# Layer 2's depthwise filter with two accumulators to a step, evictions by rows and a projection in PSUM order

## The chip, the cores and the metric

The kernel runs on one core of one Trainium2 chip. The metric is device time in microseconds of one execution of the whole program, which is four layers long. The change lies in the third of them, called layer 2 in the code. The engines have short names in the profile: PE is TensorE (PEld its weight loads), DVE is VectorE, ACT is ScalarE, POOL is GpSimd and SP is SyncE, which issues the DMAs.

## What is computed

A batch of 32 images of 96 channels and 56 x 56 pixels goes through four residual layers, each behind a group normalisation. Layer 2 is a quantized inverted bottleneck: a 1x1 convolution from 96 to 576 channels, a depthwise 3x3 convolution, and a 1x1 convolution back to 96, with 4-bit weights and activations.

```python
h = bn(conv(x, quant_w(w1, BITW), b1, 1, 0, 1), g1, be1, m1, v1)
h = act_q(h, BITA)
h = bn(conv(h, quant_w(w2, BITW), b2, 1, 1, HID), g2, be2, m2, v2)
h = act_q(h, BITA)
h = bn(conv(h, quant_w(w3, BITW), b3, 1, 0, 1), g3, be3, m3, v3)
return x + h
```

Here `act_q` clips to 0..1 and rounds to fifteenths. The kernel carries the activations as integers 0 to 15 in bf16: an eviction from PSUM applies the folded normalisation and rounds to int16, and a second instruction (`clip`) clamps to 0..15 and turns int16 into bf16 in place.

## The kernel before

The 576 channels of the bottleneck are 18 groups of 32, which make four blocks of four groups and a half block (k = 4) of two. Per image, layer 2 has these steps, each named by a letter.

- `s`, `u`, `v`, `x` and `h`, `y`, `i`, `l`: the image's statistics and normalisation, and its split into three bf16 parts (`hi`, `mid`, `lo`). `h` (L1092) and `i` (L1098) run on ACT; `x` (L1089), `y` (L1095) and `l` (L1101) on DVE. The three parts have one buffer each, so they are an order among themselves: `h`, `y`, `i`, `l`.
- `e` with k and g (expand, L1121): 24 products of a 96 x 32 weight with 392 columns, three parts by two halves by four phases. A phase is one of the four combinations of even and odd rows and columns; phase f goes to PSUM partitions 32f to 32f + 31. So a plane holds, for each group, four phases of 32 channels on 128 partitions. The even and odd halves of its columns lie in the two banks of a PSUM tile.
- `m` with k: the clip of the plane of block k (DVE, L1131).
- `a` with k and i (depthwise, L1151): the filter. A product multiplies all four phases of one group with a 128 x 32 matrix of taps; another half of the products takes only the 64 partitions of the rows above or below. Before the change there are four steps to a block (two halves of the image by even and odd output columns) and two to the half block: 18 steps an image of 32 products each. A step has one PSUM tile; its two banks are even and odd output rows. 16 of its products have 128 rows and 16 have 64.
- `n` with k: the clip of the filtered block (DVE, L1131).
- `j` with i (project, L1169) and `d` with i (add): three projections an image of 40 products, 32 with 128 rows and 8 with the 64 rows of the half block. A PSUM bank is written in the order row, column, column parity, while its layout has the parity outermost. The add is four DVE instructions (L1186) that scale the result into the image.
- `r`, `b`, `o`: residual, its factors, and statistics and store of the result.

The helper `evict` (L1112) empties a PSUM tile after `e` and after `a`: 784 float32 per partition into int16, on ACT or, for steps named in `L2_ON_DVE`, on DVE. That set is empty before.

The order on PE, DVE and ACT is written out by hand: `L2_ORDER` is a string of steps that the program walks once per image. A step with one `-` is done for the image before, with two for the one before that, with `+` for the next. Each engine executes its instructions in this order, and semaphores between them are put in by the framework.

All PSUM of layer 2 is four tiles of two banks each. The helper `bank` hands them out in strict rotation to expand, filter, projection and the two small statistics products, so the fifth request waits until the first tile is emptied. In SBUF there are five planes, six filtered blocks, two of each for the half block, and three pairs of images. After `o` of an odd image, SP stores the pair and then loads the pair after next into the same buffer.

Of the kernel before, what the change touches and what calls it, by code (L numbers as in the profile page):

```python
# [11 lines left out]
BF16 = mybir.dt.bfloat16  # L12
F32R = mybir.dt.float32r
I16 = mybir.dt.int16
# [8 lines left out]
MID = 576  # L23
NBLK = 5
SEH = 24
RT = 7
# [862 lines left out]
class Layer2:  # L889


    def __init__(self, ctx, tc, S, w, y1):
# [21 lines left out]
        def staged(p, n):  # L914
# [2 lines left out]
            return self.pairs[1].rearrange("p r i q -> p (r i q)")[:p, at[0] - n : at[0]]  # L917

        raw = [(name, staged(p, n), tile(f"{name}m", [p, 1]), tile(f"{name}a", [p, 1])) for name, p, n in (
            ("l2_w1", C, MID), ("l2_wphase", 128, NGR * NM), ("l2_w3", 128, NBLK * C))]  # L920
        taps, used, eye4 = raw[1][1], staged(128, NM), staged(128, GC)

        def load():
# [69 lines left out]
def layer2(ctx, tc, S, k2, y1, y2, norm3):  # L993
# [57 lines left out]
    def plane(im, k):  # L1051
        return planes[(CC * im["b"] + k) % L2_PLANES] if k < CC else halfplanes[im["b"] % 2]
# [54 lines left out]
    def evict(out, ps, s, o, c, step):  # L1107

        if step in L2_ON_DVE:
            nc.vector.tensor_scalar(out, ps, s[:, c : c + 1], o[:, c : c + 1], ALU.mult, ALU.add)  # L1110
        else:
            nc.scalar.activation(out, ps, AF.Identity, bias=o[:, c : c + 1], scale=s[:, c : c + 1])  # L1112

    def expand(im, k, g):

        ps, n = bank("ps"), QUAD * k + g
        for part in (hi, mid, lo):
            v = part.rearrange("c (t p r a) q -> c p a t r q", t=NP, p=NPH, a=2)
            for j in range(2):
                for f in range(4):  # L1120
                    nc.tensor.matmul(  # L1121
                        ps[f * GC : (f + 1) * GC, j, :NT].rearrange("p (t r q) -> p t r q", t=NP, q=W4),
                        w1[:, n * GC : (n + 1) * GC], v[:, f % 2 + 2 * j, f // 2],
                        start=(part is hi), stop=(part is lo),
                    )
# [7 lines left out]
    def activate(im, k):  # L1133
        clip(plane(im, k))

    def depthwise(im, k, i):

        half, p = i // 2, i % 2
        parts = [(g, half) for g in range(QUAD)] if k < CC else [(g, h) for h in range(2) for g in range(2)]
        ps, planes = bank("psd"), plane(im, k).rearrange("p g (m q) -> p g m q", q=W2)  # L1140
        q = (-1, 1)[p]
        top, bottom, every = slice(0, HALF), slice(HALF, 128), slice(128)
        rounds = [[(r, 2 * r + p, every, 0, 0)] for r in range(2)] + [[(r, 4 + 2 * r + p, every, 0, q)] for r in range(2)]
        rounds += [[(0, n, bottom, -1, dq), (1, n, top, 1, dq)] for n, dq in ((8 + p, 0), (10 + p, q))]
        n = HH // 2
        for x, products in enumerate(rounds):
            for at, (g, part) in enumerate(parts):
                for r, m, rows, dm, dq in products:
                    r0, r1 = max(part * n, -dm), min((part + 1) * n, HH - dm)
                    q0, q1 = max(0, -dq), W2 - max(0, dq)  # L1150
                    nc.tensor.matmul(  # L1151
                        ps[at * GC : (at + 1) * GC, r, :NT].rearrange("p (r w) -> p r w", w=W2)[
                            :, r0 - part * n : r1 - part * n, q0:q1],
                        filt[rows, (QUAD * k + g) * NM + m, :], planes[rows, g, r0 + dm : r1 + dm, q0 + dq : q1 + dq],
                        start=(x < 2), stop=(x == len(rounds) - 1),
                    )
        evict(act(im, k)[:, half * HH : (half + 1) * HH].bitcast(I16).rearrange("c (m r) (q p) -> c p r m q", r=2, p=2)[:, p],
              ps[:, :, :NT].rearrange("c r (m q) -> c r m q", q=W2), s2, o2, k, f"a{k}{i}")

    def activate2(im, k):  # L1160
        clip(act(im, k))
# [1 line left out]
    def project(im, i):  # L1163
        ps = im["ps"][i] = bank("psj")

        def strip(s, t, k, p, r0, **ends):
            n, c = (i, s) if s < LAST else (LAST, i)
            v = act(im, k)[p, r0 + n // 2 * 2 * RT : r0 + (n // 2 + 1) * 2 * RT]
            nc.tensor.matmul(  # L1169
                ps[s * GC : (s + 1) * GC, t, :NT].rearrange("c (m r q) -> c r q m", m=2, q=W4),  # L1170
                w3[p, k, c * GC : (c + 1) * GC], v.rearrange("p r (q j m) -> p j r q m", j=2, m=2)[:, n % 2], **ends)

        for t in range(2):
            for k in range(CC):
                for s in range(LAST + 1):
                    strip(s, t, k, slice(128), t * HH, start=(k == 0), stop=False)
        for s in range(LAST + 1):
            for t in range(2):
                strip(s, t, CC, slice(t * HALF, (t + 1) * HALF), 0, start=False, stop=True)
# [222 lines left out]
def layouts(a):  # L1402
# [28 lines left out]
    def phase_taps(v):  # L1431
# [43 lines left out]
        "l2_w3": doubled(a[i2 + "w3"].reshape(C, MID).T),  # L1475
# [32 lines left out]
```

## Time and profile before

| | |
|---|---|
| median of three runs | 5905.45 us (5895.33 to 5912.31) |
| the profiled execution | 5899.44 us, span 5897.6 us |
| mean granted TensorE clock | 0.981 |
| PE busy | 5571.7 us, 94% of the span |
| ACT busy | 4501.2 us, 76% |
| DVE busy | 4579.4 us, 78% |
| first and last product of expand (L1121) | 3612.6 and 5375.0 us |
| first and last product of the filter (L1151) | 3653.2 and 5403.9 us |
| last projection (L1169) starts | 5414.8 us |

The span runs from the first to the last instruction. Layer 2 takes roughly 3610 to 5424 us of it; layers 0 and 1 lie before, layer 3 behind. A PE product is shown with a modelled end, and four products for different groups of 32 columns of the array run side by side, so a mean duration of 330 ns says little of the pace; the distances between starts do.

### The profile page before, as it was taken

What the parts mean: (1) busy time and instruction counts of PE and PEld (TensorE: products, weight loads), DVE (VectorE), ACT (ScalarE), POOL (GpSimd) and SP (SyncE); (2) the same over time, 40 slices, a digit from 0 to 9 for tenths busy, and PEclk for the clock granted to TensorE, in tenths of its full rate; (3) what the DMA queues carried; (4) which work ended last, traced back from release to release, by engine and by line L of the source; (5) the groups of instructions that cost most, each with busy time, mean ns of one, the idle gap of its engine ahead of it and who ended that gap; (6) DMA issues with size and microseconds to landing.
All of it is one profiled execution on the core that took longest, in us unless ns stands there. A gap on an engine that the chain in (4) does not pass through costs nothing.

```text
span 5897.6 us, 159737 instructions
## 1 busy us (share of the span) xinstructions
PE 5571.7 (94%) x71208; PEld 2670.0 (45%) x71208; DVE 4579.4 (78%) x4899; ACT 4501.2 (76%) x6036; POOL 260.7 (4%) x141
## 2 busy tenths in 40 slices
PE   5999999999999999996999997999999999996899
PEld 2333333333333333333566664554554555553444
DVE  6999999999999999984766664665666666564777
ACT  5888888888888888864555655888888888895555
POOL 5000000000000000001000000000000000000000
PEclk9999999999999999997999998999999999998999
DMA  3122233322222222236587667467876876745888
GB/s 98 18 56 56 60 62 57 59 58 56 53 56 49 49 53 52 42 26 115 140 154 147 149 148 49 31 40 47 51 41 45 50 44 40 52 31 34 232 251 242
DMA packets 1306642, 455.58 MB, mean 77 GB/s; under 512 B 1123857, under 2 KB 1302025, under 8 KB 1304033
## 3 DMA queue, kind: packets, MB, share of 16 engines
q1 hardware_dynamic: 1305953, 445.36, 50.3%
q8 instruction: 558, 9.14, 0.7%
q14 instruction: 131, 1.07, 0.1%
HBM read 284.26 MB, written 214.08 MB: 84 GB/s over the span
## 4 chain that ended last, share of the span: by engine, by line
PE 88%; DMA 4%; DVE 3%; issue 2%; ACT 1%; SPq 1%; POOL 1%; ACTq 0%; DVEq 0%; POOLq 0%
PE psd L434 17%; PE psd L1151 12%; PE ps L1121 11%; PE psj L485 10%; PE ps L367 7%; PE pc L844 7%; PE pse L390 6%; PE psj L1169 5%; PE pc L1300 3%; PE pc L828 2%; DMA raw<-tdiff 2%; PE pa L802 2%; PE pc L818 1%; DMA X<-y 1%; PE pc L842 1%
## 5 line engine op out<-in xcount | busy, mean ns | idle before, releaser
L408 DVE SCALAR_TENSOR_TENSOR h<-hpad,l_wdw,h 128x3136 f32<-128x3136 f32 x512 | 1782.3, 3481 | 9.1
L434 PE MATMUL psd<-plane,filt 128*32 128x392 f32 (+5 forms) x16384 | 1082.9, 485 | 0.0
L1112 ACT ACTIVATE plane<-ps,o,s 128x784 int16<-128x784 f32 x512 | 601.6, 1249 | 141.3 <-PE ps L1121 136.6
L1151 PE MATMUL psd<-plane,filt 128*32 128x392 bf16 (+5 forms) x16384 | 673.1, 331 | 38.3 <-issue 35.0
L434 PEld LDWEIGHTS psd<-plane,filt 128*32 128x32 f32 (+1 forms) x16384 | 389.7, 108 | 674.6 <-issue 621.8
L1112 ACT ACTIVATE act<-psd,o,s 128x784 int16<-128x784 f32 x512 | 632.5, 1250 | 76.1 <-PE psd L1151 72.4
L674 ACT COPY T<-raw 32x112 f32<-32x112 f32 (+2 forms) x1440 | 463.0, 385 | 286.9 <-DMA raw<-tdiff 231.0
L1121 PEld LDWEIGHTS <-l_w1q 96*32 96x32 bf16 x13824 | 448.4, 95 | 243.0 <-issue 143.8
L1151 PEld LDWEIGHTS <-filt 128*32 128x32 bf16 (+1 forms) x18432 | 312.1, 92 | 453.1 <-issue 390.0
L367 PE MATMUL ps<-xn,l_wboth 96*128 96x392 f32 (+1 forms) x1536 | 465.8, 505 | 23.7 <-ACT xn L349 23.0
L408 DVE SCALAR_TENSOR_TENSOR hc<-hhalf,l_wdw,hc 128x1568 f32<-128x1568 f32 x256 | 473.8, 1851 | 16.1 <-ACT hc L401 9.4
L1300 PE MATMUL pc<-x,T 128*112 128x416 f32 (+1 forms) x1152 | 415.5, 523 | 53.5 <-DMA X<-y 50.7
L844 PE MATMUL pc<-x,T 128*112 128x416 f32 (+1 forms) x1152 | 445.1, 522 | 0.0
L390 PE MATMUL pse<-xn,l_wboth 96*32 96x392 f32 x4096 | 392.4, 501 | 4.6 <-ACT hab L411 4.6
L1121 PE MATMUL ps<-lo,l_w1q 96*32 96x392 bf16 x4608 | 356.3, 337 | 15.9 <-issue 13.1
L1121 PE MATMUL ps<-mid,l_w1q 96*32 96x392 bf16 x4608 | 346.9, 336 | 24.2 <-issue 18.6
L1186 DVE SCALAR_TENSOR_TENSOR xt<-psj,s,xt 32x392 f32<-32x392 f32 (+1 forms) x384 | 223.8, 621 | 177.1 <-PE psj L1169 175.4
L1121 PE MATMUL ps<-hi,l_w1q 96*32 96x392 bf16 x4608 | 339.9, 338 | 21.0 <-issue 13.1
L367 PEld LDWEIGHTS ps<-xn,l_wboth 96*128 96x128 f32 (+1 forms) x1536 | 219.4, 173 | 248.8 <-issue 59.3
L411 ACT ACTIVATE hab<-psd,o,s 128x784 f32<-128x784 f32 x256 | 284.4, 1115 | 58.5 <-PE psd L434 55.6
L1300 PEld LDWEIGHTS pc<-x,T 128*112 128x112 f32 x1152 | 203.7, 177 | 264.8 <-issue 241.4
L377 ACT ACTIVATE hpad<-ps,o,s 128x784 f32<-128x784 f32 x256 | 278.7, 1105 | 49.8 <-PE ps L367 48.5
(233 smaller groups left out, 7843.5 us busy)
## 6 DMA issues: line engine op xcount, KB each, us to landing
X<-y SPq DMA_DIRECT2D x192, 392.0 KB
y<-xt SPq DMA_DIRECT2D x180, 392.0 KB
xt<-in_x_dram SPq DMA_DIRECT2D x16, 2352.0 KB
y<-y SPq DMA_DIRECT2D x96, 392.0 KB
xt<-y SPq DMA_DIRECT2D x96, 392.0 KB
out_dram<-y SPq DMA_DIRECT2D x96, 392.0 KB
twav<-zwav SPq DMA_DIRECT2D x768, 36.8 KB
raw<-twav SPq DMA_DIRECT2D x96, 168.0 KB
```

The source lines that it names most:

```text
L367: nc.tensor.matmul(ps[p, j, :NT], wexp[:, k * 128 : k * 128 + 128][:, m], im["xn"][:, j, rows, :].rearrange("c h w -> c (h w)"), start=Tru ...
L390: nc.tensor.matmul(ps[f * GC : (f + 1) * GC, half, :NT].rearrange("p (r w) -> p r w", w=W2), wexp[:, c : c + GC], im["xn"][:, f % 2, r0 : ...
L408: nc.vector.scalar_tensor_tensor(h2, taken(im, k, t), wdw[:, k, t : t + 1], h2, ALU.mult, ALU.add)
L434: nc.tensor.matmul(ps[at * GC : (at + 1) * GC, r, :NT].rearrange("p (r w) -> p r w", w=W2)[:, r0 - half * n : r1 - half * n, q0:q1], filt[ ...
L485: nc.tensor.matmul(ps[s * GC : (s + 1) * GC, t, :NT].rearrange("c (m r q) -> c r q m", m=2, q=W4), wg[p, k, c * GC : (c + 1) * GC], phases ...
L674: nc.scalar.copy(to.rearrange("x t (p s) -> x t p s", p=NPH), v[:, k])
L844: nc.tensor.matmul(ps[:PH, to], st["T"][j][:, h, k, :], st["x"][:, j, h, of], start=False, stop=(n == NK - 1))
L1112: nc.scalar.activation(out, ps, AF.Identity, bias=o[:, c : c + 1], scale=s[:, c : c + 1])
L1121: nc.tensor.matmul(ps[f * GC : (f + 1) * GC, j, :NT].rearrange("p (t r q) -> p t r q", t=NP, q=W4), w1[:, n * GC : (n + 1) * GC], v[:, f % ...
L1151: nc.tensor.matmul(ps[at * GC : (at + 1) * GC, r, :NT].rearrange("p (r w) -> p r w", w=W2)[:, r0 - part * n : r1 - part * n, q0:q1], filt[ ...
L1169: nc.tensor.matmul(ps[s * GC : (s + 1) * GC, t, :NT].rearrange("c (m r q) -> c r q m", m=2, q=W4), w3[p, k, c * GC : (c + 1) * GC], v.rear ...
L1300: nc.tensor.matmul(ps[:, :, to], st["T"][:, h, k, :], st["x"][:, h, :, of], start=(n == 0), stop=(n == NK - 1))
```

## The change

The third weight gets a sixth block, and zeros are written so that block 4 has values for the upper 64 partitions only and block 5 for the lower 64. The filter step takes a block and a half of the image, both column parities and both row parities: it has two PSUM tiles, one for even and one for odd output rows, and in each a bank for even and one for odd columns. First come 32 products with 128 rows, then 32 with 64 rows, upper and lower in turn. There are two evictions after it, one for each tile, which read the banks in turn and write whole rows. Expand's eviction also reads its two banks in turn and writes contiguously. The projection reads the filtered block in PSUM's order, so that a product's columns are written one after the other, and takes the half block with 128 rows against the zero-filled weights. Four of the 18 expand evictions of an image go to DVE. The hand-written order is another one.

```diff
 L2_ORDER = """
-    n4-- s m3-- m4- n0-- a21-- e21- e00- u e32- e02- n2-- a32-- a33-- e01- e13- v e23- a31-- a30-- e30-
-    e22- n1-- n3-- e11- e20- e03- e12- j2-- e33- r- x m2- e31- m1- h j0-- d2-- a40- m0- d0-- a11- y a03-
-    a41- i j1-- d1-- b a23- a20- a00- a10- a22- l a01- a12- e41 e40 o-- a02- e10 a13-
+    e13- e33- m0- n4-- n1-- n0-- e41- x e20- m2- e11- n3-- e12- v n2-- e30- e40- e10- h m1- a00- a10-
+    j0-- m3- y i d0-- m4- j1-- a01- d1-- j2-- a20- d2-- a21- a30- l e00 a40- e02 r- e03 s+ a31- e01 e31
+    a11- e22 o-- u+ e21 b e23 e32
 """
 L2_PLANES, L2_ACTS = 5, 6
-L2_ON_DVE = set()
+L2_ON_DVE = {"e00", "e10", "e20", "e30"}
...
-        w1, w3 = tile("l2_w1q", [C, MID], BF16), tile("l2_w3q", [128, NBLK, C], BF16)
+        w1, w3 = tile("l2_w1q", [C, MID], BF16), tile("l2_w3q", [128, NBLK + 1, C], BF16)
...
+            nc.vector.memset(w3[64:, CC, :], 0.0)
+            nc.vector.memset(w3[:64, NBLK, :], 0.0)
...
-        evict(plane(im, k)[:, g, :].bitcast(I16).rearrange("p (m q j) -> p j m q", q=W4, j=2),
-              ps[:, :, :NT].rearrange("p j (m q) -> p j m q", q=W4), s1, o1, n, f"e{k}{g}")
+        evict(plane(im, k)[:, g, :].bitcast(I16).rearrange("p (n j) -> p n j", j=2),
+              ps[:, :, :NT].rearrange("p j n -> p n j"), s1, o1, n, f"e{k}{g}")
...
-    def depthwise(im, k, i):
+    def depthwise(im, k, half):
...
+        ps, planes = [bank("psd") for _ in range(2)], plane(im, k).rearrange("p g (m q) -> p g m q", q=W2)
+        n, sides = HH // 2, (slice(HALF, 128), slice(0, HALF))
...
+        banks = [(r, p) for r in range(2) for p in range(2)]
+        for shifted in range(2):
+            for r, p in banks:
+                for at in range(4):
+                    product(r, p, at, 4 * shifted + 2 * r + p, slice(128), 0, (-1, 1)[p] * shifted, start=not shifted)
+        for shifted in range(2):
+            for p in range(2):
+                for at in range(4):
+                    for r in range(2):
+                        product(r, p, at, 8 + 2 * shifted + p, sides[r], (-1, 1)[r], (-1, 1)[p] * shifted, stop=bool(shifted))
+        for r in range(2):
+            v = act(im, k)[:, half * HH + r : (half + 1) * HH : 2].bitcast(I16)
+            evict(v.rearrange("c m (q p) -> c m q p", p=2), ps[r][:, :, :NT].rearrange("c p (m q) -> c m q p", q=W2),
+                  s2, o2, k, f"a{k}{half}{r}")
...
-                ps[s * GC : (s + 1) * GC, t, :NT].rearrange("c (m r q) -> c r q m", m=2, q=W4),
-                w3[p, k, c * GC : (c + 1) * GC], v.rearrange("p r (q j m) -> p j r q m", j=2, m=2)[:, n % 2], **ends)
...
+                    v = act(im, k)[:, r0 : r0 + 2 * RT].rearrange("p r (q j m) -> p j m r q", j=2, m=2)[:, n % 2]
+                    nc.tensor.matmul(
+                        ps[s * GC : (s + 1) * GC, t, :NT].rearrange("c (m r q) -> c m r q", m=2, q=W4),
+                        w3[:, k + t * (k == CC), c * GC : (c + 1) * GC], v, start=(k == 0), stop=(k == CC))
```

`product` in the new filter step is the old inner product: the same tap matrix, the same shifted window of the plane, written to tile `r`, bank `p`, partitions 32 `at` on.

More of the change, by code (lines that the diff above doesn't have):

```diff
@@ L919, in __init__ @@
         raw = [(name, staged(p, n), tile(f"{name}m", [p, 1]), tile(f"{name}a", [p, 1])) for name, p, n in (
-            ("l2_w1", C, MID), ("l2_wphase", 128, NGR * NM), ("l2_w3", 128, NBLK * C))]
+            ("l2_w1", C, MID), ("l2_wphase", 128, NGR * NM), ("l2_w3", 128, (NBLK + 1) * C))]
         taps, used, eye4 = raw[1][1], staged(128, NM), staged(128, GC)
@@ L1134, in activate @@
         clip(plane(im, k))
-    def depthwise(im, k, i):
-        half, p = i // 2, i % 2
+    def depthwise(im, k, half):
         parts = [(g, half) for g in range(QUAD)] if k < CC else [(g, h) for h in range(2) for g in range(2)]
[L1140 to L1158, printed above, removed]
@@ new lines, in depthwise, with product @@
+        ps, planes = [bank("psd") for _ in range(2)], plane(im, k).rearrange("p g (m q) -> p g m q", q=W2)
+        n, sides = HH // 2, (slice(HALF, 128), slice(0, HALF))
+        def product(r, p, at, m, rows, dm, dq, start=False, stop=False):
+            g, part = parts[at]
+            r0, r1 = max(part * n, -dm), min((part + 1) * n, HH - dm)
+            q0, q1 = max(0, -dq), W2 - max(0, dq)
+            nc.tensor.matmul(
+                ps[r][at * GC : (at + 1) * GC, p, :NT].rearrange("p (r w) -> p r w", w=W2)[
+                    :, r0 - part * n : r1 - part * n, q0:q1],
+                filt[rows, (QUAD * k + g) * NM + m, :], planes[rows, g, r0 + dm : r1 + dm, q0 + dq : q1 + dq],
+                start=start, stop=stop)
@@ L1164, in project @@
         ps = im["ps"][i] = bank("psj")
[L1166 to L1169, printed above, removed]
-                ps[s * GC : (s + 1) * GC, t, :NT].rearrange("c (m r q) -> c r q m", m=2, q=W4),
-                w3[p, k, c * GC : (c + 1) * GC], v.rearrange("p r (q j m) -> p j r q m", j=2, m=2)[:, n % 2], **ends)
         for t in range(2):
-            for k in range(CC):
+            for k in range(NBLK):
                 for s in range(LAST + 1):
[L1176 to L1179, printed above, removed]
+                    n, c = (i, s) if s < LAST else (LAST, i)
+                    r0 = t * HH * (k < CC) + n // 2 * 2 * RT
+                    v = act(im, k)[:, r0 : r0 + 2 * RT].rearrange("p r (q j m) -> p j m r q", j=2, m=2)[:, n % 2]
+                    nc.tensor.matmul(
+                        ps[s * GC : (s + 1) * GC, t, :NT].rearrange("c (m r q) -> c m r q", m=2, q=W4),
+                        w3[:, k + t * (k == CC), c * GC : (c + 1) * GC], v, start=(k == 0), stop=(k == CC))
     def add(im, i):
@@ L1474, in layouts @@
         "phase_used": phase_taps(np.ones((GC, 9), np.float32))[:, 0],
-        "l2_w3": doubled(a[i2 + "w3"].reshape(C, MID).T),
+        "l2_w3": doubled(a[i2 + "w3"].reshape(C, MID).T)[:, [0, 1, 2, 3, 4, 4]],
         "l2_mid": np.concatenate([columns([i2 + n + x for n in ("b", "g", "be", "m", "v")], f) for x, f in
```

## The prediction

> **What bounds the kernel now.** I read the page's engine table and slices first, then the three 100 us windows in the middle of layer 2, then the groups of layer 2 by line, and last the timeline of TensorE (PE) over one stretch of an image. The slices show where layer 2 lies: from the 25th to the 37th, where PE and ACT are both high.
>
> ```profile
> PE   5999999999999999996999997999999999996899
> ...
> ACT  5888888888888888864555655888888888895555
> ...
> DMA  3122233322222222236587667467876876745888
> ```
>
> The windows, which show microseconds busy and instructions in brackets, put sizes to it: PE 94%, ACT 87%, DVE 63%, TensorE's clock at full.
>
> ```profile
> 4300.00:4400.00 100.00, 95.86 (x2059) 51.28 (x2053) 67.62 (x98) 87.15 (x70) 1.15 (x1) 1.00 0.84 50
> ...
> sum 300.00, PE 283.24 PEld 149.01 DVE 188.94 ACT 260.39 POOL 5.73; mean PE 94.41 PEld 49.67 DVE 62.98 ACT 86.80 POOL 1.91
> ```
>
> A busy PE is not yet a PE at its peak, so I take its work from distances between starts in the timeline.
>
> ```profile
> 4309.41 2.89 PE L1169 MATMUL psj<-act,l_w3q 128*32 128x392 bf16 x32
> 4312.23 0.52 PE L1169 MATMUL psj<-acth,l_w3q 64*32 64x392 bf16 x8
> 4312.68 1.30 PE L1151 MATMUL psd<-planeh,filt 128*32 128x392 bf16 x32
> ...
> 4320.82 8.72 PE L1151 MATMUL psd<-plane,filt 128*32 128x392 bf16 x224
> 4329.47 0.53 PE L1121 MATMUL ps<-hi,l_w1q 96*32 96x392 bf16 x8
> ...
> 4331.51 1.20 PE L1151 MATMUL psd<-plane,filt 128*32 128x392 bf16 x24
> ```
>
> The reader is to see three paces. Two expand steps (48 products) take 4331.51 - 4329.47 = 2.04 us: 0.170 us for each four products of 392 columns, which run together in four column groups. A projection takes 4312.68 - 4309.41 = 3.27 us for 40 products; its 32 full ones take 2.82 us, 0.352 us for four, twice the pace of expand. Seven filter steps of 32 products take 4329.47 - 4320.82 = 8.65 us, 1.236 us each.
>
> One image of layer 2 is, on PE: 18 expands of 1.02 (18.4), 18 filter steps of 1.236 (22.2), 3 projections of 3.27 (9.8), two small group products (0.5), together 50.9 us. The line of L1092, which runs once per image, starts first at 3615.1 and last at 5320.5: 31 intervals of 55.0 us. So 4.1 us per image are stalls. ACT has per image, from these groups, 1390.0/32 = 43.4 us of evictions (the two below and the two of the half blocks, 80.1 and 75.8), 2.9 of L1092 and 2.8 of L1098: 49.1 us. DVE, summing its layer 2 rows, has 1144/32 = 35.8 us.
>
> ```profile
> L1112 ACT ACTIVATE act<-psd,o,s 128x784 int16<-128x784 f32 x512 | 632.5, 1250 | 76.1 <-PE psd L1151 72.4 <-ACT act L1112 0.3
> L1112 ACT ACTIVATE plane<-ps,o,s 128x784 int16<-128x784 f32 x512 | 601.6, 1249 | 141.3 <-PE ps L1121 136.6 <-ACT act L1112 0.2 <-PE pv L1076 0.2
> L411 ACT ACTIVATE hab<-psd,o,s 128x784 f32<-128x784 f32 x256 | 284.4, 1115 | 58.5 <-PE psd L434 55.6
> ...
> L394 ACT ACTIVATE plane<-pse,o,s 128x784 f32<-128x784 f32 x256 | 256.1, 1001 | 26.2 <-PE pse L390 21.4
> ```
>
> ```profile
> L1186 DVE SCALAR_TENSOR_TENSOR xt<-psj,s,xt 96x392 f32<-96x392 f32 x192 | 110.9, 618 | 175.4 <-PE psj L1169 175.4
> ```
>
> These are groups by shape: busy, mean ns of one, idle time before it and what ended that. ACT and DVE wait for PE here, not PE for them: PE bounds layer 2, ACT is 2 us per image behind it.
>
> [...]only the projection writes PSUM with neighbours far apart (its innermost index steps 196 floats), and only it runs at 0.352 instead of 0.170. [...]a filter step is four quads of full products and two octets of 64-row products, six slots of 0.167 us (1.00 us) if the octets run as one; it takes 1.236, so 0.234 is left for its two changes of mode. [...]the new projection reads bf16 at steps of 8 bytes[...], and no row of before shows such a read. [...]
>
> **The change part by part.**
> Filter steps. Two steps become one of 64 products with two accumulators: eight quads, four octets, one pair of mode changes. 12 x 0.167 + 0.234 = 2.24 us against 2.47, 9 times an image: -2.1 us on the path. The 64-row products run side by side already (unpaired, the step would hold 8 slots, 1.33 us, more than it takes)[...].
> Projection. 40 full products with contiguous writes; the half block's 64-row products become 128-row ones against zeros, eight in two slots, without a change of mode. 10 x 0.167 = 1.67 against 3.27, 3 times: -4.8 us. If the 8-byte reads run at half pace, 10 x 0.33 = 3.3 and the gain is nil[...]. I take full pace, [...]the trace ties the slow pace to the writes.
> PE then: 50.9 - 6.9 = 44.0 us.
> Evictions. Both forms now write int16 rows contiguously (before: every second element) and read the two PSUM banks in turn. Contiguous writing is worth up to 249 ns (1250 against L394). What reading in turn costs no row shows: at the least nothing (1001)[...]. I take 0.1, the price that a strided far side has in L411 (1115 against 1001): 1.1 us. Four of 36 evictions per image go to DVE. ACT: 32 x 1.1 + 5.7 = 40.9 us, where unchanged evictions would give 45.7.
> DVE. Four tensor_scalars of 784 floats from PSUM: from L1186, 618 ns for 392, plus 392 more at 1.04 ns (L408's two sizes, 3481 ns for 3136 and 1851 for 1568), an estimate of 1.03 us[...]. 35.8 + 4.1 = 39.9 us, beside PE. Behind each stand clips, the chain rest and lo, and the projection's adds; e00 stands right behind lo, which PE needs for e00 anyway.
> Banks. A filter step now holds two of the four tiles for 2.24 us and both evictions start at its end, so the second tile is held 2.24 + 2.2 us; before, 1.24 + 1.25. Time that tiles are held per image: before 18 x 2.27 (expand) + 18 x 2.49 + 3 x 5.6 (projection and its adds of 2.35) = 103 of 4 x 55 us; after 18 x 2.1 + 9 x (3.3 + 4.4) + 3 x 4.0 = 119 of 4 x 49. Between the last expand of one image and the first of the next, PE has 6 filter steps and 3 projections, 18.4 us; DVE, from the end of L1092 (2.9), must do L1095 (3.46), three adds of 2.35, a clip and L1101 (3.41), 17.4 us in all. It fits with 1 us to spare; the stretch of before was 20.1 us (two projections, 11 filter steps). For both I add 0.9 us of stalls per image.
> Once-only edits (a wider third weight, two memsets) are under 1 us beside layer 1.
> DMA: a pair's store and load take 4211.45 to about 4282, some 70 us, of the 110 us of two images; at 98 us it still fits.
>
> Sum: 44.0 + 4.1 + 0.9 = 49.0 us against 55.0; 6.0 x 32 images = -192 us. The profiled execution took 5899.4 (span 5897.6), 6 us under the median of 5905.5. 5899.4 - 192 = 5707; I say 5705.
>
> **The rivals.**
> A, the reads of the projection are slow (half pace): PE 48.8, stalls as before, 52.9 us: -2.1 x 32 = -67; with ACT's relief taking a little more, 5820. For it: nothing in before reads so.[...]
> B, the stalls shrink, as ACT is 8 us per image lighter and no longer close behind PE: 44.0 + 2 = 46 us, -288: 5610. For it: ACT, busy 49.1 of 55.0, is the only engine near PE, so its bursts are the nearest cause of PE's stalls. Against: the tiles are held longer.
> C, slower: reading PSUM banks in turn costs ACT more than contiguous writing saves. It decides from (55.0 - 4.1 - 5.7)/32 = 1.41 us an eviction; at 1.55 ACT has 55.3 us, with stalls 59: +4 x 32 = 6030. For it: the 0.25 us that strided writing costs shows that ACT is not indifferent to steps. Against: f32 at 8-byte steps cost only 0.1.
> D, two tiles per filter step starve PE: stalls rise to about 11 us and the interval stays at 55: 5895, no change.
> That the pairs were meant to run together for the first time is excluded above.
>
> **How the numbers follow.** Forecast 0.50, A 0.17, B 0.14, C 0.13, D 0.06. Predicted: 5705. The range reaches from B's side, 5600, to just past A, 5840; C, D and a little of B's tail lie outside. 0.3% (18 us) is about what a measurement of this kernel can tell from no change. Faster: 0.50 + 0.17 + 0.14 = 0.81; same: most of D, 0.04; slower: C and the rest of D, 0.15.
>
> **What would show it.** In the changed profile: four products of L1169's successor at 0.17 us pace, a projection of 1.7 us (A: 3.3); a filter step of 2.2 us with one gap of about 0.1 us before its 64-row part; evictions at 1.0 to 1.15 us (C: over 1.4) and DVE evictions at about 1.0; hi starting every 49 us. PE waiting for evictions rather than the reverse, with ACT under 85%, would show D. The prediction is wrong if evictions come out above 1.3 or the projection above 2.2.

## The result, and the profile after

The changed kernel takes 5930.78 us (median; 5914.36 to 5952.28), the kernel before in the same runs 5911.09 us (5895.33 to 5922.98). The ratio is 1.0039, with a 95% interval of 1.0027 to 1.0051: 0.4% slower, where 3.4% faster was forecast. The profiled execution took 5931.0 us (span 5929.2).

The slices of the page hardly differ for PE and DMA; ACT is lighter in layer 2.

```profile
PE   5999999999999999986999997999899999896899
...
ACT  5888888888888888864565654666566666663455
...
DMA  3122233222222222236576666556956866745888
```

The three windows in the middle of layer 2 for which the prediction shows before (microseconds busy, instructions in brackets; clock, DMA share and GB/s at the end) say the same with sizes.

```profile
4300.00:4400.00 100.00, 92.88 (x2008) 57.80 (x2004) 67.51 (x93) 64.98 (x61) 2.29 (x2) 1.00 0.61 43
...
sum 300.00, PE 277.18 PEld 172.81 DVE 198.72 ACT 189.57 POOL 6.87; mean PE 92.39 PEld 57.60 DVE 66.24 ACT 63.19 POOL 2.29
```

ACT went from 87% to 63%, DVE from 63% to 66%, PE from 94% to 92%. PE runs 2008 products in the first of these windows, before it ran 2059. PE still bounds the layer and waits more often. Each eviction, by shape (busy, mean ns, idle before and what ended it), is as cheap as was hoped:

```profile
L1114 ACT ACTIVATE act<-psd,o,s 128x784 int16<-128x784 f32 x512 | 486.2, 1000 | 412.7 <-PE psd L1148 408.0 <-issue 3.9
L1114 ACT ACTIVATE plane<-ps,o,s 128x784 int16<-128x784 f32 x384 | 376.7, 1005 | 103.2 <-PE ps L1123 96.5
```

1000 and 1005 ns stand against 1250 and 1249; the 128 evictions on DVE (L1112) take 1092. The fault lies on PE. Its timeline (start, length, products in the row) over a projection and over three filter steps:

```profile
4323.81 1.58 PE L1181 MATMUL psj<-act,l_w3q 128*32 128x392 bf16 x16
4325.20 0.54 PE L1181 MATMUL psj<-acth,l_w3q 128*32 128x392 bf16 x4
...
4327.31 1.63 PE L1181 MATMUL psj<-act,l_w3q 128*32 128x392 bf16 x16
...
4336.58 6.87 PE L1148 MATMUL psd<-plane,filt 128*32 128x392 bf16 x192
4343.38 0.53 PE L1123 MATMUL ps<-hi,l_w1q 96*32 96x392 bf16 x8
```

A projection takes 4327.31 - 4323.81 = 3.50 us for 40 products, ten quads (four products side by side) of 0.350 us: the pace of before, not 0.167. Three filter steps of 64 products take 4343.38 - 4336.58 = 6.80, 2.27 us each. PE's work per image is then 18.4 (expand, unchanged) + 9 x 2.27 + 3 x 3.50 + 0.5 = 49.8 us, before 50.9. The line of L1092, now L1094, runs once per image; its row gives shortest, median and longest duration, then first and last start:

```profile
L1094 ACT ACTIVATE hi<-xt,rstd x32: 2897/2917/2931, 3615.4 to 5344.4; 96x3136 bf16<-96x3136 f32 x32
```

That is 1729.0/31 = 55.8 us per image, before 55.0. So 1.1 us of work went and 1.9 us of stalls came: 6.0 us against 4.1. Over 31 intervals +24 us; from the last `hi` to the last projection the pipeline now runs dry in 107.7 us instead of 94.2, another +13. The remainder of the profiled difference, a few us the other way, lies outside layer 2.

What is a stall? The view of PE's waits over 3750 to 5150 us (released by; us in total, times, longest) answers "issue", a wait that no semaphore ends. First before, then after:

```profile
PE ps L1121 <- issue: 37.3, 42, 2.7
PE psd L1151 <- issue: 32.5, 35, 3.0
```

```profile
PE psd L1148 <- issue: 59.2, 42, 4.7
PE ps L1123 <- issue: 37.5, 33, 5.7
...
PE psd L1148 <- DVE plane L1133: 2.7, 17, 0.2
PE psd L1148 <- ACT act L1114: 2.6, 1, 2.6
```

In these rows evictions (L1114) and clips (L1133) hold PE for 5.3 of 1400 us; "issue" holds it for 97, before for 70. Where such waits fall is seen in the timeline:

```profile
4347.84 0.35 PE L1148 MATMUL psd<-planeh,filt 64*32 64x378 bf16 x7 [1.18 <-issue]
4348.12 0.53 PE L1123 MATMUL ps<-hi,l_w1q 96*32 96x392 bf16 x8
...
4349.81 0.58 PE L1123 MATMUL ps<-lo,l_w1q 96*32 96x392 bf16 x8
4350.15 2.38 PE L1148 MATMUL psd<-plane,filt 128*32 128x392 bf16 x64
4352.46 0.53 PE L1123 MATMUL ps<-hi,l_w1q 96*32 96x392 bf16 x8
4352.81 0.33 PE L1123 MATMUL ps<-mid,l_w1q 96*32 96x392 bf16 x1
4355.15 0.53 PE L1123 MATMUL ps<-mid,l_w1q 96*32 96x392 bf16 x7 [2.01 <-issue]
```

Between the two gaps stand 7 + 48 (six rows of expand, of which the first and the last are shown) + 64 + 8 + 1 = 128 products. The second gap cuts a run of eight equal products after the first, where no data can be late. Along the whole layer two gaps are 128 products apart or a multiple of it, give or take the one or two that the trace may miss. A product is two instructions (a weight load and a matmul: 2004 and 2008 of them in the first window above), so 128 are 256 instructions. The page counts PE's instructions and, for one DMA queue of the kind "instruction", packets and MB:

```profile
PE 5563.7 (94%) x71208; PEld 2777.3 (47%) x71208; DVE 4711.7 (79%) x5029; ACT 4119.9 (69%) x5908; POOL 255.5 (4%) x141
...
q8 instruction: 558, 9.14, 0.7%
```

That is 9.14/558 MB = 16.4 KB (16384 bytes) a packet, and 2 x 71208/558 = 255 of PE's matmuls and weight loads to a packet; the other engines together have far fewer instructions than that. So q8's packets are read here as blocks of 256 of PE's instructions, and a gap falls where one block ends; the gaps are up to 5.7 us long. The DMA view of the same window has the blocks (packets, MB, share), and its slices of 2.5 us show when data moves:

```profile
DMA  9000000000000001556545555565555899999999
GB/s 47 4 7 0 7 0 7 0 0 7 0 7 0 0 7 17 59 59 73 64 57 70 62 66 63 61 75 63 67 64 63 95 67 66 70 68 68 62 63 70
...
q1 hardware_dynamic: 35866, 4.00, 59.8%
q8 instruction: 15, 0.25, 1.1%
...
y<-xt SPq DMA_DIRECT2D x6, 392.0 KB
xt<-y SPq DMA_DIRECT2D x5, 392.0 KB
```

Fifteen blocks are what 2008 products need (2008/128 = 15.7). From 4303 to 4337 us no image is moved: the lone sevens are instruction blocks, one every 4 to 8 us, and the products of that stretch, the projections above among them, run without a gap over 0.2 us. From 4338 the store of a pair of images runs, six transfers of 392 KB in a row, and the gaps begin, 6.2 to 7.3 us apart where one comes at each edge.

The trace also has the time of each block. SP issues the second and third of these transfers at 4345.00 and 4351.86 us; blocks start at 4345.49 and 4352.80 and take 0.9 us each, and PE goes on at 4347.84 and 4355.15. Over the whole layer it is the same: every one of the 82 gaps (counted as in the next section) ends 1.2 to 2.5 us after a block has landed, and of the 133 blocks that start while SP is issuing an image transfer (for 6.3 us, as a rule) 110 start in its first 2 us, where chance would give about a third.

A part of the stalls is no wait at all. From the first to the last `hi`, TensorE's granted clock stands at half for 100.6 us in all, before for 39.8. In both, 19 us of that lie at the layer's beginning; the rest comes in stretches of 3.4 or 6.8 us, 16 of them after and 5 before. Four expand products take 0.327 us there instead of 0.170. This is one, with the gap in front of it and a filter step that takes 3.6 us, mostly inside it, and then a window of it (the 0.50 is the clock):

```profile
4404.03 0.85 PE L1148 MATMUL psd<-plane,filt 64*32 64x364 bf16 x28 [2.55 <-issue]
...
4406.11 3.68 PE L1148 MATMUL psd<-planeh,filt 128*32 128x392 bf16 x64
4409.72 0.53 PE L1123 MATMUL ps<-hi,l_w1q 96*32 96x392 bf16 x8
```

```profile
4405.60:4408.80 3.20, 3.20 (x44) 1.83 (x36) 2.37 (x2) 1.22 (x2) 0.00 (x0) 0.50 1.61 67
```

Ten of the 16 begin within 1.6 us after the end of a distance of over 2 us between the starts of two products, the other six in the last 1.7 us of one; past the layer's beginning after has 24 of them. At half clock PE loses half the time: 1.6 us per image after, 0.6 before. So of the 1.9 us by which the stalls grew, about half are gaps (3.0 to 4.0, the table below) and half are clock.

### The profile page after: what moved, and what is told of

The parts are those of the page before. It is cut to its first block, busy times and chain, and to the rows that moved or that the text cites. A ratio compares the mean times of both kernels' runs of the same rounds, so it can differ in the third digit from the quotient of the medians.

```text
span 5929.2 us, 159802 instructions
## 1 busy us (share of the span) xinstructions
PE 5563.7 (94%) x71208; PEld 2777.3 (47%) x71208; DVE 4711.7 (79%) x5029; ACT 4119.9 (69%) x5908; POOL 255.5 (4%) x141
## 3 DMA queue, kind: packets, MB, share of 16 engines
q8 instruction: 558, 9.14, 0.7%
## 4 chain that ended last, share of the span: by engine, by line
PE 86%; DVE 4%; DMA 3%; issue 3%; SPq 2%; ACT 1%; POOL 1%; DVEq 0%; ACTq 0%; POOLq 0%
PE psd L434 17%; PE ps L1123 11%; PE psj L485 10%; PE psd L1148 10%; PE ps L367 7%; PE pc L844 7%; PE pse L390 6%; PE psj L1181 6%; PE pc L1304 3%; PE pc L828 2%; PE pa L802 2%; DMA raw<-tdiff 1%; PE pc L818 1%; DVE h L408 1%; PE pc L842 1%
## 5 line engine op out<-in xcount | busy, mean ns | idle before, releaser
L1114 ACT ACTIVATE act<-psd,o,s 128x784 int16<-128x784 f32 x512 | 486.2, 1000 | 412.7 <-PE psd L1148 408.0
L1148 PE MATMUL psd<-plane,filt 128*32 128x378 bf16 (+5 forms) x16384 | 619.1, 330 | 51.9 <-issue 43.4
L1123 PEld LDWEIGHTS <-l_w1q 96*32 96x32 bf16 x13824 | 475.2, 97 | 227.2 <-issue 137.2
L1148 PEld LDWEIGHTS <-filt 128*32 128x32 bf16 (+1 forms) x18432 | 416.3, 95 | 352.7 <-issue 250.5
L1114 ACT ACTIVATE plane<-ps,o,s 128x784 int16<-128x784 f32 x384 | 376.7, 1005 | 103.2 <-PE ps L1123 96.5
L1123 PE MATMUL ps<-lo,l_w1q 96*32 96x392 bf16 x4608 | 380.6, 342 | 24.1 <-issue 21.4
L1123 PE MATMUL ps<-mid,l_w1q 96*32 96x392 bf16 x4608 | 373.7, 343 | 15.7 <-issue 10.1
L1123 PE MATMUL ps<-hi,l_w1q 96*32 96x392 bf16 x4608 | 367.9, 345 | 21.7 <-issue 16.6
L411 ACT ACTIVATE hab<-psd,o,s 128x784 f32<-128x784 f32 x256 | 284.0, 1114 | 58.8 <-PE psd L434 55.8
L1181 PE MATMUL psj<-act,l_w3q 128*32 128x392 bf16 x3072 | 310.9, 528 | 7.1 <-DVE act L1133 4.4
```

Source lines behind the costliest of these rows:

```text
L1123: nc.tensor.matmul(ps[f * GC : (f + 1) * GC, j, :NT].rearrange("p (t r q) -> p t r q", t=NP, q=W4), w1[:, n * GC : (n + 1) * GC], v[:, f % ...
L1148: nc.tensor.matmul(ps[r][at * GC : (at + 1) * GC, p, :NT].rearrange("p (r w) -> p r w", w=W2)[:, r0 - part * n : r1 - part * n, q0:q1], fi ...
L1181: nc.tensor.matmul(ps[s * GC : (s + 1) * GC, t, :NT].rearrange("c (m r q) -> c m r q", m=2, q=W4), w3[:, k + t * (k == CC), c * GC : (c + ...
```

## The experiments

Theory F (fetch): a block of PE's instructions waits behind a transfer of image data that is under way, so while images are moved PE gets 128 products per transfer, about 6.4 us, however fast it works. Expand uses 128 x 42.5 ns = 5.4 us for a block, the old filter step 4.95, the new one 4.5: what PE wins in such a stretch it waits for at the block's edge. Rivals: T, the two tiles held by a filter step (or the evictions) make PE wait; O, the new hand-written order does; for the projection, W, that before was slow through its scattered writes and after is slow through its reads at 8-byte steps. The table has the median of each version, its ratio to the kernel before run beside it, the interval between starts of `hi`, and two counts from the trace per image, from the first to the last `hi`. "Gaps" adds up the distances of over 0.55 us between the starts of two successive products, less 0.17 us each, where the second waits for no semaphore. "Half clock" is half the time at half clock, idle time in it included.

| version | us | ratio (95%) | interval | gaps | half clock |
|---|---|---|---|---|---|
| before | 5911.09 | 1 | 55.0 | 3.0 | 0.6 |
| after | 5930.78 | 1.0039 (1.0027 to 1.0051) | 55.8 | 4.0 | 1.6 |
| b_big | 5958.53 | 1.0099 (1.0084 to 1.0114) | 55.1 | 2.6 | 1.9 |
| a_big | 6000.63 | 1.0174 (1.0157 to 1.0191) | 56.0 | 4.2 | 2.7 |
| b_halves | 5790.53 | 0.9810 (0.9795 to 0.9824) | 51.8 | 0.55 | 0.3 |
| a_split | 5788.28 | 0.9816 (0.9799 to 0.9833) | 51.5 | 1.2 | 0.3 |
| b_split4 | 5777.88 | 0.9774 (0.9755 to 0.9793) | 51.3 | 0.17 | 0.3 |
| a_split4 | 5763.11 | 0.9748 (0.9724 to 0.9772) | 50.7 | 0.4 | 0.3 |
| a_fours | 5820.68 | 0.9867 (0.9851 to 0.9884) | 52.0 | 4.5 | 1.3 |
| a_fours_split | 5676.09 | 0.9619 (0.9604 to 0.9634) | 48.1 | 1.65 | 0.5 |
| a_fours_split4 | 5612.93 | 0.9501 (0.9478 to 0.9524) | 46.0 | 0.17 | 0.3 |
| a_oldorder | 5912.48 | 1.0021 (1.0009 to 1.0032) | 55.4 | 2.5 | 1.2 |
| a_oldproj | 5905.78 | 0.9997 (0.9982 to 1.0011) | 54.7 | 4.1 | 1.6 |
| a_nodve | 5934.76 | 1.0051 (1.0036 to 1.0066) | 55.4 | 3.8 | 1.3 |
| b_evict | 5910.81 | 1.0012 (1.0001 to 1.0023) | 55.6 | 3.2 | 1.2 |

Names with a_ start from the kernel after, those with b_ from the kernel before.

**Long runs instead of short ones (a_big, b_big).** The image transfers consist of packets of 112 bytes (4.00 MB in 35866 packets on q1 in the window above). If the fetch waits behind many small packets, one run of 25 KB per channel should free it. These kernels move other images' pixels than asked, from the fourth pair on, and store likewise; the bytes are the same.

```diff
+    def flat(y, b, n):
+        return y.rearrange("c r b q -> c (r b q)")[:, b * HW : (b + n) * HW]
...
-                for to, of in groups(pair, y1, lambda y: y[:, :, b : b + 2, :]):
-                    nc.sync.dma_start(to, of)
+                for to, of in groups(pair, y1, lambda y: y):
+                    if b < 6:
+                        nc.sync.dma_start(to, of[:, :, b : b + 2, :])
+                    else:
+                        nc.sync.dma_start(to.rearrange("c r i q -> c (r i q)"), flat(of, b, 2))
...
```

> The changed kernel, with layer 2's loads (from the fourth pair of images on) and stores as one run of 25 KB per channel instead of runs of 112 bytes; the same bytes, but pixels of other images, so the result is not the reference's. Theory F (PE's instructions arrive in blocks of 256, and while a load or store of short runs is under way only one block comes per transfer, about 6.4 us, where PE needs 5 to 5.5 us for one): the gaps every 128 products go, the interval between images falls from 55.8 to 50 to 51 us, the total to about 5770. Theory T (two PSUM tiles to a filter step starve PE): the interval stays at 55 or more and the total at 5900 or more.

> The kernel before with the same long runs. F: the interval falls from 55.0 to 51 to 52 us (50.9 of work), total about 5790, so that the changed kernel with long runs is faster than this one by about 1 us per image. T: falls less than 1 us, and the changed one stays slower than this one by 20 us or more.

Both are slower. The gaps are fewer (36 of them against 82 after, 34 against 85 before) and longer, and their sum hardly changes (4.2 against 4.0 us, 2.6 against 3.0). a_big, PE and then SP:

```profile
4371.34 0.56 PE L1129 MATMUL ps<-hi,l_w1q 96*32 96x392 bf16 x4
4379.81 0.51 PE L1129 MATMUL ps<-hi,l_w1q 96*32 96x392 bf16 x2 [7.91 <-issue]
```

```profile
4362.43 2.71 SPq L1029 DMA_DIRECT2D xt<-y  x6
```

Six transfers are issued within 2.7 us (after: one per 6.4 us), and PE stands for 7.91 us. All six have been issued by 4365.14 us, but no block starts between 4361.83 and 4376.72. So F as first put, with the number of packets as the cause, fell; what was left of it is the reading that a block waits for the bytes that stand in front, issued or not. Most of the added time (by the ratios 80 us in a_big, 58 in b_big) is elsewhere: from layer 2's last projection to the end both are 52 us longer, and why is open.

**Shorter transfers (a_split, b_halves, a_split4, b_split4).** Each load and store of a pair is cut by rows into n = 2 or 4; bytes, runs and everything else stay (n stands for the number in the code).

```diff
-                for to, of in groups(pair, y1, lambda y: y[:, :, b : b + 2, :]):
-                    nc.sync.dma_start(to, of)
+                for r in range(0, H * NPH, H * NPH // n):
+                    rows = slice(r, r + H * NPH // n)
+                    for to, of in groups(pair[:, rows], y1, lambda y: y[:, rows, b : b + 2, :]):
+                        nc.sync.dma_start(to, of)
...
-        store_images(nc, y2, im)
+        for r in range(0, H * NPH, H * NPH // n):
+            store_images(nc, y2, im, slice(r, r + H * NPH // n))
```

> The changed kernel with each of layer 2's loads and stores split into two transfers of 112 rows. F: a block of instructions waits for a transfer half as long (3.3 us, less than a block lasts), the gaps shrink to a third, interval 51 to 53 us, total about 5830. T, or a fetch that waits for the queue as a whole: no change, 5925.

> The kernel before with its loads and stores split in two. F: its gaps of 3.0 us per image fall to about 1.0, interval 53.5, total about 5835, above the changed kernel with split transfers (5788) by 20 to 50 us: the filter's gain shows once the gaps are gone. If the gaps are the changed kernel's own: 5890 or more.

> The kernel before with its loads and stores split in four. With the gaps at the ends of 128 products gone, the interval is PE's work and what else holds PE up: F 50.9 + 1 = 52.0 us, total about 5775. If something else (tiles, evictions) stands behind the gaps: 5790, as with two.

> The changed kernel with its loads and stores split in four. F: 49.8 + 1 = 50.8 us an image, total about 5740, some 35 us below the kernel before with the same split, which is then what the change is worth in PE's work (filter less, projection more). T (two tiles to a step starve PE once the gaps are gone): no faster than the kernel before with the same split, 5775 or more.

By the ratios, two halves give after 132 us and before 112; four parts 172 and 133. The waits of the same 1400 us are, in a_split4 and then in b_split4:

```profile
PE ps L1125 <- issue: 8.5, 12, 2.0
PE psd L1150 <- DVE plane L1135: 4.7, 24, 1.0
PE psd L1150 <- issue: 3.2, 9, 0.6
PE ps L1125 <- ACT act L1116: 0.7, 2, 0.4
PE psd L1150 <- ACT act L1116: 0.2, 1, 0.2
```

```profile
PE ps L1123 <- issue: 1.9, 3, 1.2
PE psd L1153 <- issue: 1.6, 2, 1.3
PE psj L1171 <- issue: 0.8, 1, 0.8
```

After, "issue" fell from 97 to 12 us. This is F's main evidence, together with the times of the blocks: no instruction of PE, ACT or DVE in layer 2 was touched. With the gaps went the stretches at half clock, but for the one at the layer's beginning and at most one more. The miss: b_halves came out level with a_split, where F, counting PE's work alone, put it 20 to 50 us above. At four parts the changed kernel is 15 us ahead (its slowest run took 5770 us, the fastest of the other 5775), where its 1.1 us less work would give 35. Of stalls a_split4 keeps 50.7 - 49.8 = 0.9 us per image by the first and last start, b_split4 51.3 - 50.9 = 0.4. The rows above hold that half microsecond: some 0.3 us are "issue", 0.2 are waits for the clip of a plane. For evictions, which would set a PSUM tile free, PE waits 0.9 us in all of the 1400. So T explains next to nothing. The end of the layer costs another 7 us, 97.7 against 90.2 from the last `hi` to the last projection. Half a microsecond in 31 intervals and these 7 us are about the 20 us that are missing.

**What slows the projection (a_forms).** Six forms of the same 40 products in one kernel, one form for each of the three projections of even and of odd images. Which pixels are multiplied, and where they land, differs between the forms, so most of layer 2's projection is not the reference's. `apart` and `twos` are the write and the read of before, `whole` and `eights` those of after.

```diff
+                    eights = v.rearrange("p r (q j m) -> p j m r q", j=2, m=2)[:, n % 2]
+                    twos = v.rearrange("p r (q j m) -> p j r q m", j=2, m=2)[:, n % 2]
+                    fours = v.rearrange("p r (m q j) -> p j m r q", j=2, m=2)[:, n % 2]
+                    runs = v.rearrange("p r (j m q) -> p j m r q", j=2, m=2)[:, n % 2]
+                    line = v.rearrange("p r w -> p (r w)")[:, :NT]
+                    o = ps[s * GC : (s + 1) * GC, t, :NT]
+                    apart = o.rearrange("c (m r q) -> c r q m", m=2, q=W4)
+                    whole = o.rearrange("c (m r q) -> c m r q", m=2, q=W4)
...
```

> The changed kernel with six forms of projection, three on even images and three on odd ones; its result is not the reference's, as pixels are mixed. Pace of four products. Theory W (strided writes to PSUM set the pace before, reads in steps of 8 bytes set it after): pairs of bf16 read, written together 0.17 us; 392 in line read, written apart 0.33; in line and together 0.17; steps of 4 bytes 0.17 to 0.33; runs of 14 read 0.17; steps of 8 bytes 0.35. Theory R (reads set it in both): pairs read, written together 0.33; in line, written apart 0.17; the rest as W.

The groups of PE by shape (mean ns after the busy time):

```profile
L1193 PE MATMUL psj<-act,l_w3q 128*32 128x392 bf16 x496 | 52.1, 555 | 6.5 <-issue 6.5
L1201 PE MATMUL psj<-act,l_w3q 128*32 128x392 bf16 x480 | 47.9, 528 | 0.0
...
L1195 PE MATMUL psj<-act,l_w3q 128*32 128x392 bf16 x512 | 27.2, 331 | 2.4 <-issue 1.5 <-DVE xt L1208 0.9
```

By the distances between starts, a quad takes:

| form | us per quad |
|---|---|
| read in line, written together (L1195) | 0.166 |
| read in pairs as before, written together (L1191) | 0.175 |
| read in runs of 14 (L1199), written together | 0.180 |
| read at 4-byte steps (L1197), written together | 0.198 |
| read in line, written apart as before (L1193) | 0.329 |
| read at 8-byte steps as after (L1201), written together | 0.3485 |

W holds: the change took away one cause of half pace and put another in its place.

**A projection that both reads and writes well (a_fours, a_fours_split, a_fours_split4).** The filter's evictions lay each row out as its even, then its odd columns, which lets the projection read at 4-byte steps and still write together; then the same with transfers in two and in four.

```diff
-            evict(v.rearrange("c m (q p) -> c m q p", p=2), ps[r][:, :, :NT].rearrange("c p (m q) -> c m q p", q=W2),
+            evict(v.rearrange("c m (p q) -> c p m q", p=2), ps[r][:, :, :NT].rearrange("c p (m q) -> c p m q", q=W2),
...
-                    v = act(im, k)[:, r0 : r0 + 2 * RT].rearrange("p r (q j m) -> p j m r q", j=2, m=2)[:, n % 2]
+                    v = act(im, k)[:, r0 : r0 + 2 * RT].rearrange("p r (m q j) -> p j m r q", j=2, m=2)[:, n % 2]
```

> The changed kernel, with the filter's evictions writing each row's even columns and then its odd ones (the banks one after the other), so that the projection reads bf16 in steps of 4 bytes instead of 8 and still writes PSUM in order. Projection 40 x 0.198/4 = 2.0 us instead of 3.5: PE's work per image falls from 49.8 to 45.3. If PE's work bounds the interval, it falls by 4.5 us and the total to about 5790. Theory F: part is given back in longer gaps at the ends of 128 products, since blocks of instructions come no faster; interval 53.5, total about 5825.

> The same with loads and stores split in two. F: both gains add up, 45.3 us of work and 2.6 of stalls, interval 48 to 49 us, total about 5680. If PE is no longer the bound (DVE has 40 us per image), 50 us and 5740.

> The version with reads in steps of 4 bytes, its loads and stores split in four instead of two. F: a block of instructions waits behind a quarter of a transfer; the gaps of 1.65 us per image fall below 0.8, interval 48.0, total about 5650. If the transfers' own fixed costs count: loads land late, 5676 or more.

The timeline of a_fours_split4 has the projection at 4303.28 - 4301.25 = 2.03 us:

```profile
4301.25 0.99 PE L1183 MATMUL psj<-act,l_w3q 128*32 128x392 bf16 x16
...
4303.28 0.98 PE L1183 MATMUL psj<-act,l_w3q 128*32 128x392 bf16 x16
```

PE's work is then 49.8 - 3 x 1.47 = 45.4 us. With whole transfers (a_fours) the interval is 52.0, so stalls are 6.6 us. In four parts the row of `hi` gives 46.0, stalls 0.6, and PE is 99% busy from 4300 to 4700 us:

```profile
L1096 ACT ACTIVATE hi<-xt,rstd x32: 2899/2915/2938, 3615.3 to 5041.7; 96x3136 bf16<-96x3136 f32 x32
```

```profile
sum 400.00, PE 396.66 PEld 270.83 DVE 333.89 ACT 307.24 POOL 9.16; mean PE 99.17 PEld 67.71 DVE 83.47 ACT 76.81 POOL 2.29
```

This version takes 5612.93 us, 5% less than before, and beats both kernels.

**One part of the change at a time (a_oldorder, a_oldproj, a_nodve, b_evict).** The changed steps in the order of before, with four expand evictions still on DVE; the change with the projection of before; the change with `L2_ON_DVE` empty; and before with only expand's eviction in its new form.

```diff
 L2_ORDER = """
...
+    n4-- s m3-- m4- n0-- a20-- e21- e00- u e32- e02- n2-- a31-- e01- e13- v e23- a30-- e30- e22- n1-- n3--
+    e11- e20- e03- e12- j2-- e33- r- x m2- e31- m1- h j0-- d2-- m0- d0-- a10- y a01- a40- i j1--
+    d1-- b a21- l a00- e41 e40 o-- e10 a11-
```

> The changed steps in the order of before (each pair of filter steps done where its second one stood; four expand evictions still on DVE). Theory O (the new order makes the end longer and the gaps fall worse): the time from the last L1094 to the last projection goes back from 108 to about 95 us, total 5905 to 5915. F with tiles: the order of before was not made for two tiles to a step, so stalls grow, total 5940 or more.

```diff
...
+                w3[p, k + t * (k == CC), c * GC : (c + 1) * GC], v.rearrange("p r (q j m) -> p j r q m", j=2, m=2)[:, n % 2], **ends)
...
```

> The changed kernel with the projection of before (pairs of bf16 read, PSUM written apart, 64-row products for the half block): 3.27 us instead of 3.50. PE's work falls by 0.7 us per image, 22 us; total about 5910, and with it most of the loss against before is gone. If the projection's slower pace is covered by gaps that would otherwise come: no change, 5930.

```diff
-L2_ON_DVE = {"e00", "e10", "e20", "e30"}
+L2_ON_DVE = set()
```

> The changed kernel with all expand evictions on ACT: ACT has 4 us more per image, 42 of 56, DVE 4.4 less. If ACT and DVE are both off the path: no change, 5920 to 5940. If expand's evictions on DVE, queued behind its long steps, cost PE waits: faster, 5900 or less. If ACT was relieved where it counts: 5960 or more.

```diff
-        evict(plane(im, k)[:, g, :].bitcast(I16).rearrange("p (m q j) -> p j m q", q=W4, j=2),
-              ps[:, :, :NT].rearrange("p j (m q) -> p j m q", q=W4), s1, o1, n, f"e{k}{g}")
+        evict(plane(im, k)[:, g, :].bitcast(I16).rearrange("p (n j) -> p n j", j=2),
+              ps[:, :, :NT].rearrange("p j n -> p n j"), s1, o1, n, f"e{k}{g}")
```

> The kernel before with only expand's eviction in the new form (banks read in turn, int16 written in line). These evictions on ACT fall from 1249 to 1005 ns, 18 x 0.244 = 4.4 us of ACT's 49.1 per image. If ACT does not hold PE up in the kernel before: no change, within 10 us of 5903. If its stalls come from bursts of evictions (the prediction's rival B): interval down by 1 to 2 us, total 5840 to 5870.

a_oldproj: 25 us less than after (medians of different runs; ratios 0.9997 and 1.0039). In before's form the projection takes 3.27 us (3.20 at the median in a_oldproj), in the new one 3.50: 96 x 0.23 = 22 us. So the new projection explains the loss by itself, and all else in the change, 1.8 us per image of filter work and lighter evictions, comes to nothing against before: its gaps and its time at half clock are those of after (4.1 and 1.6 us), and so is its long drain (106.3 us). b_evict: an ACT lighter by a quarter microsecond 18 times per image gains nothing (1.0012). a_nodve: the DVE evictions don't matter in either direction. a_oldorder: the old order is some 11 us better on the ratios (their intervals just overlap). Its drain at the end of the layer is 98.2 us, near before's 94.2. From 3750 to 5150 us it waits on semaphores for 27 us, 15.6 of them for `lo`, where after waits for 7.5, but its gaps come to 2.5 us per image against 4.0. So O is right in a small part: the new order costs a longer drain, and what it saves in waits on semaphores doesn't show in the interval, 55.8 against 55.4.

## Why the prediction was wrong

It fell at two steps of its sum, 49.0 us per image, measured 55.8.

- **The projection's term (1.67 us), "I take full pace".** Measured 3.50, three times per image: 5.5 of the 6.8 us. No row of before had such a read, so full pace was the author's estimate. The runs show a graded price: 8-byte steps of bf16 0.3485 us a quad, 4-byte steps 0.198, in line 0.166. That the slow pace of before was tied to its writes was right (a_forms: read in line, 0.329 written apart and 0.166 together), and no reason for the new reads to be fast. Half pace stood there as the other end and as rival A, which is what happened. A's "3.3, the gain is nil" was still too kind: the half block's eight products, formerly side by side in 0.45 us, are now two quads at the slow pace, 0.70 us, which is the 0.23 us.
- **The stalls, 4.1 + 0.9 us, carried over as if they were a fixed toll.** Measured 6.0, the last 1.0 us of the difference, and with a fast projection they are 6.6 (a_fours). They were not asked for their cause: the view of waits would have said "issue". Of their growth over before about half are gaps at the edges of instruction blocks and half is time at half clock; waits on semaphores are 0.7 us per image in both. Rival B took them for ACT's bursts: ACT is now busy 63% of the windows and the stalls grew, and b_evict, with a lighter ACT alone, gained nothing. Were the projection's size the only error, a_fours (45.4 us of work) would have come near 5.0 + 45.4 = 50.4 us; it came to 52.0. This is why rival A's sum (52.9 us, 5820) also missed the result: PE work 48.8 (measured 49.8) with "stalls as before".

The other 0.3 us are the filter's: 2.24 predicted, 2.27 measured. In the step that starts at 4336.58 us the first octet starts 0.28 us behind the last quad, and the next step 0.32 us behind the last octet, where quads are 0.166 us apart: 0.27 us for the two changes between 128 and 64 rows, where 0.234 was put down. One such pair instead of two is what the step saves; so it is a gain of work, 1.8 us per image, that shows in the total, and then in part, only once the transfers are cut. ACT evictions, 1.1 predicted, came out at 1.00, so rival C has no ground: two banks in turn cost ACT nothing that shows beside L394's 1001 ns. DVE evictions, 1.03 predicted, took 1.09. The extra 0.9 us for tiles held longer is not found: waits for evictions hold PE for a few microseconds in 1400, in after as in a_split4. So rival D comes near the total (5895) with the wrong cause, and with stalls of 11 us where 6.0 were measured. Once-only edits are nil, the first `hi` starting at 3615.4 against 3615.1. The transfer of a pair "still fits" was the right question asked too narrowly: it was looked at for its own lateness, not for what else has to be moved at the same time.

Shown are: the spacing of 128 products, that blocks start at the edges of transfers and PE goes on when one has landed, that cutting transfers removes the gaps, that longer runs lengthen the single gap, and both causes of the projection's half pace. Argued only: why a block comes after the data in front of it; the profile has the times of both, not what decides between them. That the gaps bring on the stretches at half clock is likely, as both go together when transfers are cut and all 16 begin in a long gap or just behind it, but of the 24 long gaps eight bring on none. Open: what sets those eight apart, and why the part behind layer 2 suffered in a_big and b_big.

## What to carry to other kernels

Before stalls of a busy engine are carried into a sum as a constant, ask the view of waits what ends them; if it is nothing ("issue") and the gaps come at a fixed count of instructions (here 256), look whether the instruction stream is late; here faster work was then mostly given back until the DMAs beside it were cut shorter. Look at the granted clock of the layer too: here it was 1.0 of the 1.9 us per image that the stalls gained. In moving a stride from one side of a matmul to the other, price both sides (here 0.329 us a quad for the write, 0.3485 for the read), and prefer to let an eviction rearrange the data: it did so here for 1.00 us whatever the order of banks.

## What the runs showed of the hardware

- PE's instructions arrive in blocks of 256 (on q8, 558 packets of 16.4 KB for 142416 matmuls and weight loads); while 392 KB transfers are under way PE stands for up to 5.7 us at a block's edge, behind six of them queued at once for 7.9 (a_big); in 1400 us at 98 KB (a_split4) "issue" falls from 97 to 12.
- PE goes on 1.2 to 2.5 us after such a block has landed (82 gaps of after).
- TensorE's granted clock falls to half for stretches of 3.4 or 6.8 us, 16 times in after and, past the layer's beginning, hardly at all with 98 KB transfers (0.3 us lost per image in a_split4, the layer's beginning included, against 1.6); four expand products then take 0.327 us instead of 0.170.
- A bf16 matmul of 392 columns, four side by side: 0.166 us in line, 0.175 reading pairs, 0.198 at 4-byte steps, 0.3485 at 8-byte steps, 0.329 with a scattered PSUM write.
- An ACT eviction of 784 floats to int16 costs 1250 ns (before) to every second element and 1000 ns (after) to a contiguous row, though it then reads two PSUM banks in turn.
